# Decoder kernel: position-bias matmuls interleaved over row quarters and PSUM banks, and the residual stream held in eight fixed tiles

## The chip, the core and the metric

The kernel runs on one core of a Trainium2 chip. The core has five engines that work through their own instruction queues in order and meet at semaphores: TensorE (PE; its weight loads are shown apart as PEld), VectorE (DVE), ScalarE (ACT), GpSimd (POOL) and SyncE (SP), which here only issues DMAs. The metric is the device time of one execution in microseconds; lower is better. Three executions of the kernel before took 3527.88, 3530.78 and 3538.53 us (median 3530.78).

## What is computed

A two-layer decoder over 64 sequences of 128 positions with 256 features. Six blocks follow each other, each adding to the residual stream `x`:

```python
x = x + L0_attn(layernorm(x), ...)            # A: window-7 attention, 16 heads
x = x + L0_xattn(layernorm(x), ctx, mask, ...) # B: masked cross attention, no projections of q, k, v
x = x + L0_ffn(layernorm(x), ...)             # C: 64 slots, top-8 routing, GRU update of the slots
x = x + L1_attn(layernorm(x), ...)            # D: causal attention with a position bias
x = x + L1_xattn(layernorm(x), ctx, ...)      # E: cross attention
x = x + L1_ffn(layernorm(x), ...)             # F: ternary-weight FFN with a depthwise convolution
```

The position bias of D is one 128 x 128 table for each of 16 heads, the same for all sequences:

```python
rel = log(abs(c * (pos_t - pos_s)) + 1)
pos_norm = log(abs(c * max(pos_t, abs(512 * L_multiplier))) + 1) + 1e-6
h = relu((rel / pos_norm)[..., None] * w1[0] + b1)   # 32 hidden values for each pair (t, s)
bias = einsum('tsw,wh->hts', h, w2) + b2             # -inf where s > t
att = softmax(q @ k.T * scale + bias)
```

## The kernel before

All is float32, apart from the quantised operands of F. The 64 sequences are taken in 16 groups of four (`GB` = 4), so that a tile of the residual stream is [128 positions, 4, 256], 512 KB. Every stage reads the groups from DRAM and writes them back: A writes `ab`, B and C together write `cd`, D writes `de`, E writes `ef`, F writes the output. The class `Flow` (L61 to L80) does this. `reach(g)` makes a tile of the pool `xp` (six buffers, L1354) for each group up to `g` and issues its load on SP's queue (L77); `store(g)` issues the store there (L80). Weights and `ctx` are loaded on the same queue (L96, L578), a few broadcast rows on POOL's.

The program is not run in the order in which it is written. A scheduler places every instruction on its engine's queue by its own estimate of when its inputs are there and when buffers come free, with the order of the text as priority; after that each engine is strictly in order. So a load is placed as early as a buffer of its pool is free. With six buffers, the load of a group waits for the store of the group six before it.

Stage A (`stage_window`) works in groups. Between two of its groups it calls one preparation of a later stage at a time. One of them is `prep_fire`, which makes the bias table: `nd` holds, in each quarter of 32 partitions, the 32 hidden values for 32 of the 128 positions t and all 128 s. For each quarter q (L971) one PSUM bank is taken from the pool `ps`, 32 matmuls (L974) of a stationary 32 x 128 piece of `nd` by the moving 32 x 16 `w2` fill it, and four DVE additions (L980) move it to `bias_t`. POOL then masks it (L985), and 16 transposes (L989) make `bias_s`. A matmul in float32 runs as two instructions, so that L974 is 256 of them.

Beside this stands the window attention of A itself: `window_values` (L325) takes two tiles of two banks each from the pool `sc` (two buffers), fills them with the spread weights (L333), and DVE multiplies and sums (L339, L343).

Stage B (`stage_cross0`) is written for each sequence as `prep`, which normalises (`ln_stats`: L122 to L125, then `r` L617 and `qp` L623), and `attention_stage`, a software pipeline of half-steps shared by B, D and E: score bursts of 16 matmuls (L433, 32 instructions), exponentials on ACT (L456, L454), maxima on DVE (L460), transposes and values on PE (L471, L483, L495, L512), output (L165). In B the burst takes two row quarters for the scores of one sequence and the other two for the scores of another. Stage C, the slots, runs inside B's pipeline a step at a time (`Slots.tick`); its last additions to a group (L868) release the store to `cd`. D and E (`stage_attn`) project each group ahead of its use (`group_project`), and F (`stage_bitnet`) is a pipeline over groups of its own, with DVE, POOL and ACT in turn: `hs` times a scale on POOL (L1264), rounding on DVE (L1265), convolution on PE (L1210).

Of the kernel before, what the change touches and what calls it, by code (L numbers as in the profile page):

```python
# [10 lines left out]
F = mybir.dt.float32  # L11
# [5 lines left out]
D = 256  # L17
H = 16
DH = 16
S = 128  # L20
WIN = 7
SLOTS = 64
GB = 4
# [37 lines left out]
class Flow:  # L61

    def __init__(self, k, src, dst):
        self.k, self.src, self.dst = k, src, dst
        self.at = -1
        k.x = {}
        k.flow = self

    def reach(self, g):

        k = self.k
        while self.at < min(g, k.G - 1):
            self.at += 1
            k.x[self.at] = k.xp.tile([S, GB, D], F, tag="x", name="x")
            k.nc.sync.dma_start(out=k.x[self.at], in_=self.src[self.at])  # L77

    def store(self, g):
        self.k.nc.sync.dma_start(out=self.dst[g], in_=self.k.x[g])  # L80


def outside(k, name):
# [23 lines left out]
def psum(k):  # L107
    return k.ps.tile([128, 512], F, tag="ps", name="ps")


def psum2(k):
    return k.sc.tile([128, 2, 512], F, tag="sc", name="sc")
# [460 lines left out]

def load_group(k, pool, g):
    cx = pool.tile([S, GB, D], F, tag="cx", name="cx")
    k.nc.sync.dma_start(  # L578
        out=cx, in_=k.a["ctx"][g * GB : (g + 1) * GB].rearrange("b l d -> l b d")
    )  # L580
    return cx


def stage_cross0(k, w, wc):


    nc = k.nc
    with k.tc.tile_pool(name="wb", bufs=2) as wp, k.tc.tile_pool(name="wb1", bufs=1) as w1, \
            k.tc.tile_pool(name="wb3", bufs=3) as w3, k.tc.tile_pool(name="wc2", bufs=2) as c2:
        qps, kps, vas = [], [], []  # L590
        for i in range(2):
            qp = w1.tile([S, H, 32], F, name=f"qp{i}")
            nc.gpsimd.memset(qp, 0.0)
            nc.gpsimd.memset(qp[:, :, 17:18], 1.0)
            qps.append(qp)
            kp = w1.tile([S, H, 32], F, name=f"kp{i}")
            nc.gpsimd.memset(kp, 0.0)
            nc.gpsimd.memset(kp[:, :, 16:17], 1.0)
            kps.append(kp)
        for i in range(4):  # L600
            va = w1.tile([S, H, 32], F, name=f"va{i}")
            nc.gpsimd.memset(va, 0.0)
            nc.gpsimd.memset(va[:, :, 16:17], 1.0)
            vas.append(va)
        cxs = {0: load_group(k, wp, 0)}
        k.flow.reach(0)
        stats = {}

        def prep(bi):
            g, b = divmod(bi, GB)  # L610
            if b == 0:
                k.flow.reach(g + 1)
                if g + 1 < k.G:
                    cxs[g + 1] = load_group(k, wp, g + 1)
                mv, rs = ln_stats(k, wp, g)
                r4 = wp.tile([S, GB], F, tag="r4", name="r4")
                nc.vector.tensor_scalar(r4, rs, 0.25, None, ALU.mult)  # L617
                stats[g] = mv, r4
            mv, r4 = stats[g]
            mk = w.mask[:, bi : bi + 1]  # L620
            qp, kp, va = qps[b % 2], kps[b % 2], vas[b]
            xb = k.x[g][:, b, :]
            nc.vector.tensor_scalar(  # L623
                qp[:, :, 0:DH], xb.rearrange("p (h d) -> p h d", d=DH),
                mv[:, b, 0:1], r4[:, b : b + 1], ALU.subtract, ALU.mult,
            )
            xm = wp.tile([S, D], F, tag="xm", name="xm")
            nc.gpsimd.tensor_scalar(xm, w.bp, mk, None, ALU.mult)
            nc.gpsimd.tensor_tensor(xb, xb, xm, ALU.add)
            cv = cxs[g][:, b, :].rearrange("p (h d) -> p h d", d=DH)  # L630
            nc.gpsimd.tensor_copy(kp[:, :, 0:DH], cv)
            nc.gpsimd.tensor_copy(kp[:, :, 17], w.mbias[:, bi : bi + 1].to_broadcast([S, H]))
            nc.gpsimd.tensor_scalar(va[:, :, 0:DH], cv, mk, None, ALU.mult)
            t = Batch()
            t.qt = w3.tile([128, 4, S], F, tag="qt", name="qt")
            t.kt = w3.tile([128, 4, S], F, tag="kt", name="kt")
            for src, dst in ((qp, t.qt), (kp, t.kt)):
                p = psum(k)
                sf = src.rearrange("p h i -> p (h i)")
                for c in range(4):  # L640
                    nc.tensor.transpose(
                        p[:, c * S : (c + 1) * S], sf[:, c * 128 : (c + 1) * 128], k.ident
                    )
                nc.scalar.copy(dst, p.rearrange("p (c l) -> p c l", l=S))
            t.va, t.row_scale = va, mk

            def fin(y):
                nc.vector.scalar_tensor_tensor(xb, y, mk, xb, ALU.mult, ALU.add)

            t.fin = fin  # L650
            return t

        slots = Slots(k, wc, c2, w1)
        attention_stage(k, wp, w1, prep, w.wp, Heads(False), tick=slots.tick)
        slots.finish()

# [279 lines left out]
def prep_fire(k, pool):  # L936
    nc = k.nc
    bt = pool.tile([S, 4, 4, S], F, name="bias_t")
    bs = pool.tile([S, 4, 4, S], F, name="bias_s")
    with k.tc.tile_pool(name="firew", bufs=1) as cp:  # L940
        w1 = load(k, cp, "f_w1")
        b1 = load(k, cp, "f_b1")
        w2 = load(k, cp, "f_w2")
        b2 = load_row(k, cp, "f_b2")
        c = load_row(k, cp, "f_c")
        lm = load_row(k, cp, "f_l")
        thr = cp.tile([128, 1], F, name="thr")
        nc.scalar.activation(thr, lm, AF.Abs, scale=512.0)
        pn = cp.tile([128, 32], F, name="pn")
        nd = cp.tile([128, 32, S], F, name="nd")  # L950
        for q in range(4):
            sl = slice(32 * q, 32 * q + 32)
            nc.gpsimd.iota(
                pn[sl], [[1, 32]], base=32 * q, channel_multiplier=0,
                allow_small_or_imprecise_dtypes=True,
            )
            nc.gpsimd.iota(
                nd[sl], [[1, 32], [-1, S]], base=32 * q, channel_multiplier=0,
                allow_small_or_imprecise_dtypes=True,
            )  # L960
        nc.vector.tensor_scalar(pn, pn, thr[:, 0:1], None, ALU.max)
        nc.scalar.activation(pn, pn, AF.Abs, scale=c[:, 0:1])
        nc.scalar.activation(pn, pn, AF.Ln, bias=1.0)
        nc.vector.tensor_scalar(pn, pn, 1e-6, None, ALU.add)
        nc.vector.reciprocal(pn, pn)
        nc.scalar.activation(nd, nd, AF.Abs, scale=c[:, 0:1])
        nc.scalar.activation(nd, nd, AF.Ln, bias=1.0)
        nc.vector.tensor_tensor(nd, nd, pn.unsqueeze(2).to_broadcast([128, 32, S]), ALU.mult)
        nc.scalar.activation(nd, nd, AF.Relu, scale=w1[:, 0:1], bias=b1[:, 0:1])
        b2v = b2.rearrange("p (c r) -> p r c", r=4)  # L970
        for q in range(4):  # L971
            p = psum(k)
            for t in range(32):
                nc.tensor.matmul(  # L974
                    p[:, t * H : (t + 1) * H], nd[32 * q : 32 * q + 32, t, :],
                    w2[32 * q : 32 * q + 32, :], start=True, stop=True,
                )
            pv = p.rearrange("p (t c r) -> p r c t", c=4, r=4)
            for r in range(4):
                nc.vector.tensor_tensor(  # L980
                    bt[:, r, :, 32 * q : 32 * q + 32], pv[:, r],
                    b2v[:, r, :].unsqueeze(2).to_broadcast([S, 4, 32]), ALU.add,
                )
        btf = bt.rearrange("p r c l -> p (r c) l")
        nc.gpsimd.affine_select(btf, btf, [[0, 16], [1, S]], ALU.is_ge, NEG, 0, -1)  # L985
        for r in range(4):
            p = psum(k)
            for cc in range(4):
                nc.tensor.transpose(p[:, cc * S : (cc + 1) * S], bt[:, r, cc, :], k.ident)  # L989
            nc.scalar.copy(bs[:, r], p.rearrange("p (c l) -> p c l", l=S))  # L990
    return bt.rearrange("p r c l -> p r (c l)"), bs.rearrange("p r c l -> p r (c l)")
# [351 lines left out]
def decoder(tc, a):  # L1343
    k = Ctx()
# [6 lines left out]

    with ExitStack() as ctx:
        k.res = ctx.enter_context(tc.tile_pool(name="res", bufs=1))
        k.xp = ctx.enter_context(tc.tile_pool(name="xp", bufs=6))  # L1354
        k.dram = ctx.enter_context(
            tc.tile_pool(name="flow", bufs=1, space=bass.MemoryType.DRAM)
        )
# [3 lines left out]
        p = Ctx()  # L1361
# [143 lines left out]
```

## Time and profile before

| | us |
|---|---|
| median of three executions | 3530.78 |
| the profiled execution | 3546.0 |
| its span, first to last instruction | 3544.2 |
| mean granted TensorE clock of it | 0.906 of full speed |

Busy time of each engine by stage, from windows of the trace (the stages overlap a little at their ends, so that the borders are rounded):

| stretch, us | stage | PE | DVE | ACT | POOL | TensorE clock |
|---|---|---|---|---|---|---|
| 0 to 690 | A and preparations | 545.71 | 490.27 | 98.85 | 335.51 | 0.84 |
| 690 to 1626 | B with C | 756.73 | 575.23 | 383.34 | 329.72 | 0.90 |
| 1626 to 2330 | D | 624.78 | 622.47 | 286.60 | 62.47 | 0.95 |
| 2330 to 2925 | E | 558.73 | 356.99 | 289.37 | 59.72 | 0.99 |
| 2925 to 3544 | F | 444.38 | 508.46 | 252.54 | 215.90 | 0.85 |

No engine is busy all through any stage. A busy PE is not PE at its peak: its matmuls are pipelined and their ends are modelled. The granted clock is the share of full speed that TensorE got in a stretch. The page of a profile also has rows by line of the program ("busy, mean ns of one", then the idle time of the engine just before them and what ended it), and the chain of work that ended last, followed back from the last instruction.

### The profile page before, as it was taken

To read this page: it belongs to the slowest core of one execution; us is meant where nothing else is said; L and a number is where in the kernel's file an instruction comes from. 1 tells how busy PE (TensorE), PEld (TensorE's weight loads), DVE (VectorE), ACT (ScalarE), POOL (GpSimd) and SP (SyncE) were. 2 spreads that over 40 slices of the span, in tenths; PEclk is the share of its full clock that TensorE was granted. 3 is DMA by queue.
4 is the path that set the end of the run, shared out by engine and by line. 5 is a ranking of instruction groups with operands and counts; after the bars stand their busy time and mean duration, and the time that the engine had idled before them with its cause. 6 is when DMAs were issued, how large, how long until landed. Compare 5 with 4: busy or idle time off the path is not lost.

```text
span 3544.2 us, 65123 instructions
## 1 busy us (share of the span) xinstructions
PE 2930.3 (83%) x27738; PEld 1892.7 (53%) x27764; DVE 2553.4 (72%) x4875; ACT 1310.7 (37%) x2012; POOL 1003.3 (28%) x920
## 2 busy tenths in 40 slices
PE   5869888688888878877999999879999987777776
PEld 2445333365656656654666666657777763333333
DVE  6855787666666666657988899865656559888876
ACT  1111111044444444433444444335555544434442
POOL 6434555434333333312000000030101003334323
PEclk9867999789999999988999999999999998888887
DMA  4100010100101001000000000011111110001000
GB/s 129 60 12 12 36 36 24 54 13 19 37 19 37 25 31 37 13 30 19 25 25 25 25 25 25 25 49 38 55 37 55 38 44 8 33 24 36 24 12 24
DMA packets 59249, 115.20 MB, mean 33 GB/s; under 512 B 6496, under 2 KB 39664, under 8 KB 58704
## 3 DMA queue, kind: packets, MB, share of 16 engines
q1 hardware_dynamic: 58304, 109.29, 8.9%
q8 instruction: 219, 3.59, 0.4%
q0 software_dynamic: 656, 1.75, 0.2%
q14 instruction: 70, 0.57, 0.1%
HBM read 69.08 MB, written 41.94 MB: 31 GB/s over the span
## 4 chain that ended last, share of the span: by engine, by line
PE 40%; DVE 35%; POOL 9%; ACT 7%; DMA 5%; issue 4%; SPq 0%; POOLq 0%; DVEq 0%; ACTq 0%
PE sc L433 9%; PE ps L156 7%; DVE negmax L460 5%; PE ps L165 5%; DVE uq L1265 4%; PE ps L483 3%; DVE sb L447 3%; DVE e L453 3%; PE cv L1210 2%; DVE pv L339 2%; ACT e L454 2%; DVE oT L343 2%; PE ps L1045 2%; PE ps L471 2%; POOL pr L281 2%
## 5 line engine op out<-in xcount | busy, mean ns | idle before, releaser
L433 PE MATMUL sc<-kt,qt 32*128 32x128 f32 x6144 | 519.5, 297 | 152.6 <-DVE negmax L460 97.5
L433 PEld LDWEIGHTS sc<-kt,qt 32*128 32x128 f32 x6144 | 425.1, 196 | 331.4 <-DVE negmax L460 149.2
L433 PE MATMUL sc<-q,kt 32*128 32x128 f32 x6144 | 491.5, 295 | 5.2 <-DVE q L475 2.6
L433 PEld LDWEIGHTS sc<-q,kt 32*128 32x128 f32 x6144 | 407.2, 196 | 26.5 <-DVE rec L498 11.6
L460 DVE TENSOR_REDUCE negmax<-sc 128x8 f32<-128x1024 f32 x256 | 312.4, 1220 | 138.6 <-ACT e L456 133.6
L456 ACT ACTIVATE e<-sc 128x1024 f32<-128x1024 f32 x256 | 261.5, 1021 | 324.4 <-PE sc L433 324.0
L1210 PE MATMUL cv<-hp,taps 128*128 128x512 f32 x480 | 259.6, 684 | 63.7 <-DVE hp L1200 63.4
L281 POOL TENSOR_TENSOR pr<-pad,qt 128x896 f32<-128x896 f32 x128 | 244.9, 1945 | 191.8 <-ACT pad L268 184.4
L475 DVE TENSOR_TENSOR q<-ps,qt 128x512 f32<-128x512 f32 x192 | 131.9, 687 | 154.2 <-PE ps L471 154.2
L1264 POOL TENSOR_TENSOR hs<-hs,s2b 128x512 f32<-128x512 f32 x128 | 180.0, 1441 | 198.1 <-ACT s2b L1256 198.1
L454 ACT ACTIVATE e<-e 128x1024 f32<-128x1024 f32 x128 | 135.3, 1057 | 240.7 <-DVE e L453 240.7
L447 DVE TENSOR_TENSOR sb<-sc,bias_s 128x1024 f32<-128x1024 f32 x128 | 156.6, 1223 | 66.0 <-PE sc L433 66.0
L1210 PEld LDWEIGHTS cv<-hp,taps 128*128 128x128 f32 x480 | 97.8, 215 | 191.0 <-DVE hp L1200 94.3
L125 POOL TENSOR_TENSOR ln_rs<-ln_ve,expo 128x4 f32<-128x4 f32 x96 | 101.9, 1061 | 328.8 <-DVE ln_ve L124 198.3
L122 DVE BATCH_NORM_STATS2 ln_st<-x 128x6 f32<-128x256 f32 x384 | 153.4, 425 | 56.5 <-DMA x<-ab 29.8
L339 DVE TENSOR_TENSOR pv<-sc,pad 128x896 f32<-128x896 f32 x128 | 137.0, 1083 | 77.7 <-PE sc L333 77.6
L1013 POOL TENSOR_TENSOR x<-x,t_d_bo 128x1024 f32<-128x1024 f32 x16 | 37.6, 2353 | 469.4 <-DVE xn L132 469.4
L488 ACT COPY avs<-ps 128x512 f32<-128x512 f32 x192 | 112.2, 584 | 153.7 <-PE ps L483 153.7
L1265 DVE TENSOR_SCALAR uq<-hs 128x512 bf16<-128x512 f32 x128 | 151.4, 1233 | 8.6 <-POOL hs L1264 8.6
L453 DVE TENSOR_TENSOR e<-sc,bias_t 128x1024 f32<-128x1024 f32 x128 | 155.5, 1215 | 1.3 <-PE sc L433 1.3
L460 DVE TENSOR_REDUCE negmax<-sb 128x8 f32<-128x1024 f32 x128 | 154.9, 1210 | 0.0
L333 PE MATMUL sc<-fw,spread 32*128 32x448 f32 x512 | 111.4, 648 | 50.5 <-DVE fw L322 27.7
(329 smaller groups left out, 6448.6 us busy)
## 6 DMA issues: line engine op xcount, KB each, us to landing
cx<-in_ctx_dram SPq DMA_DIRECT2D x32, 512.0 KB, 4.2
x<-in_x_dram SPq DMA_DIRECT2D x16, 512.0 KB, 3.8
ab<-x SPq DMA_DIRECT2D x16, 512.0 KB, 2.6
x<-ab SPq DMA_DIRECT2D x16, 512.0 KB, 3.2
cd<-x SPq DMA_DIRECT2D x16, 512.0 KB, 2.8
x<-cd SPq DMA_DIRECT2D x16, 512.0 KB, 3.2
de<-x SPq DMA_DIRECT2D x16, 512.0 KB, 2.6
x<-de SPq DMA_DIRECT2D x16, 512.0 KB, 3.2
```

What stands on the lines that cost most here:

```text
L156: k.nc.tensor.matmul(out, w[:, kc, c0 : c0 + cn], rhsT[:, kc, n0 : n0 + n], start=(kc == 0), stop=(kc == 1),)
L281: k.nc.gpsimd.tensor_tensor(pr[:, c], shift_windows(t.kt, b, c), t.qt[:, c, b, :].unsqueeze(1).to_broadcast([128, WIN, S]), ALU.mult,)
L339: nc.vector.tensor_tensor(pv, bc[th][:, :, 0 : WIN * 64].rearrange("p c (l w) -> p c l w", w=WIN), shift_windows2(t.vt, b, th), ALU.mult,)
L433: k.nc.tensor.matmul(t[:, side * 2 + rr, c * S : (c + 1) * S], st[rows, c, :], mv[rows, c, :], start=True, stop=True,)
L447: nc.vector.tensor_tensor(sb, src, bias_s[:, hf * 2 : hf * 2 + 2, :], ALU.add)
L453: nc.vector.tensor_tensor(e, t[:, 2:4, :], bias_t[:, hf * 2 : hf * 2 + 2, :], ALU.add)
L454: nc.scalar.activation(e, e, AF.Exp)
L456: nc.scalar.activation(e, t[:, 2:4, :], AF.Exp)
L460: nc.vector.tensor_reduce(b.lay.extra(b.nm, hf * 2), src.rearrange("p r (c m) -> p r c m", m=S), AX.X, ALU.max, negate=True,)
L1210: nc.tensor.matmul(pc, w.taps[:, CONV_PE.index(j), t, :], hp[:, :, t : t + S], start=(t == 0), stop=(t == 2),)
L1264: nc.gpsimd.tensor_tensor(hs[:, j], hs[:, j], s2b, ALU.mult)
L1265: nc.vector.tensor_scalar(uq[:, j], hs[:, j], MAGIC, MAGIC, ALU.add, ALU.subtract)
```

## The change

The bias matmuls change their order: position t runs in the outer loop and the row quarter q in the inner one, and the four quarters write four different banks, which come from the pool `sc` as two tiles of two banks. The DVE additions of all four quarters follow after the last matmul. The residual stream gets eight fixed tiles of the resident pool, which all stages use in turn, in place of the pool `xp`. A store is noted in a list and issued by the next call of `reach`, behind its load, or with the last group. In stage B, `ctx` has three buffers in place of two.

```diff
     def __init__(self, k, src, dst):
         self.k, self.src, self.dst = k, src, dst
         self.at = -1
+        self.done = []
         k.x = {}
         k.flow = self
...
         while self.at < min(g, k.G - 1):
             self.at += 1
-            k.x[self.at] = k.xp.tile([S, GB, D], F, tag="x", name="x")
+            k.x[self.at] = k.xs[k.turn % len(k.xs)]
+            k.turn += 1
             k.nc.sync.dma_start(out=k.x[self.at], in_=self.src[self.at])
+        self.flush()
 
     def store(self, g):
-        self.k.nc.sync.dma_start(out=self.dst[g], in_=self.k.x[g])
+        self.done.append(g)
+        if g == self.k.G - 1:
+            self.flush()
+
+    def flush(self):
+        for g in self.done:
+            self.k.nc.sync.dma_start(out=self.dst[g], in_=self.k.x[g])
+        self.done = []
...
-def load_group(k, pool, g):
-    cx = pool.tile([S, GB, D], F, tag="cx", name="cx")
+def load_group(k, pool, g, bufs=None):
+    cx = pool.tile([S, GB, D], F, tag="cx", name="cx", bufs=bufs)
...
-        cxs = {0: load_group(k, wp, 0)}
+        cxs = {0: load_group(k, wp, 0, 3)}
...
-                    cxs[g + 1] = load_group(k, wp, g + 1)
+                    cxs[g + 1] = load_group(k, wp, g + 1, 3)
...
-        for q in range(4):
-            p = psum(k)
-            for t in range(32):
+        ps = [psum2(k) for _ in range(2)]
+        for t in range(32):
+            for q in range(4):
                 nc.tensor.matmul(
-                    p[:, t * H : (t + 1) * H], nd[32 * q : 32 * q + 32, t, :],
+                    ps[q // 2][:, q % 2, t * H : (t + 1) * H], nd[32 * q : 32 * q + 32, t, :],
                     w2[32 * q : 32 * q + 32, :], start=True, stop=True,
                 )
-            pv = p.rearrange("p (t c r) -> p r c t", c=4, r=4)
+        for q in range(4):
+            pv = ps[q // 2][:, q % 2].rearrange("p (t c r) -> p r c t", c=4, r=4)
             for r in range(4):
                 nc.vector.tensor_tensor(
                     bt[:, r, :, 32 * q : 32 * q + 32], pv[:, r],
...
-        k.xp = ctx.enter_context(tc.tile_pool(name="xp", bufs=6))
+        k.xs = [k.res.tile([S, GB, D], F, name=f"x{i}") for i in range(8)]
+        k.turn = 0
```

## Prediction

> **What bounds the kernel now.** I read the table of stages first: no engine is full anywhere, so each stage is set by waits, and I looked for those that the edits touch. First the row of the bias matmuls and the window of the trace in which they run. The columns of a window: length, then busy time with the number of instructions for PE, PEld, DVE, ACT and POOL, then the granted TensorE clock, the DMA share and GB/s.
>
> ```profile
> L974 PE MATMUL ps<-t_f_w,nd 32*128 32x16 f32 x256 | 52.1, 369 | 0.0
> 237.00:289.00 52.00, 52.00 (x260) 52.00 (x260) 2.65 (x12) 0.00 (x0) 0.00 (x0) 0.50 0.00 1
> ```
>
> For 52 us PE works through 256 small matmuls, one every 51.31 / 256 = 0.200 us, and DVE does 2.65 us of work, ACT and POOL none. The chain of waits has 51.31 us of L974 in one piece. This stretch is wholly on the path that sets the end. The clock stays at 0.50.
>
> Next, who waits for DMAs. The row of the layer norm statistics, then the chain of waits in one group of stage B (start, us, what), then windows from one `cd` store to the next.
>
> ```profile
> L122 DVE BATCH_NORM_STATS2 ln_st<-x 128x6 f32<-128x256 f32 x384 | 153.4, 425 | 56.5 <-DMA x<-ab 29.8 <-DMA x<-de 21.1 <-DMA x<-cd 2.9
> ...
> 905.38 2.91 DMA cd<-x
> 908.29 0.02 issue
> 908.30 3.11 DMA x<-ab
> 911.41 0.02 issue
> 911.44 1.41 DVE ln_st L122 x4
> ...
> 905.40:961.40 56.00, 47.32 (x542) 35.24 (x538) 35.81 (x97) 23.85 (x39) 20.48 (x28) 0.90 0.09 29
> 961.40:1014.30 52.90, 44.49 (x558) 33.48 (x550) 35.59 (x97) 23.75 (x39) 20.62 (x28) 0.97 0.09 31
> 1014.30:1072.30 58.00, 46.88 (x550) 34.88 (x546) 35.92 (x98) 23.87 (x39) 20.47 (x28) 0.91 0.09 28
> ...
> 1412.00:1462.90 50.90, 44.52 (x554) 33.49 (x554) 34.04 (x87) 23.76 (x39) 19.55 (x27) 0.97 0.06 22
> ```
>
> The load of a group waits for the store of the group six before it, about 6 to 8 us for both, and DVE, in order, stands at L122 for it: in B ten times, 29.8 us. Behind it are queued the next `negmax` (L460), and behind that the score burst of PE. Where store and load take 5.8 us, PE keeps a clock of 0.97 and the group takes 53; where they take 6 to 8, PE idles long enough to fall to 0.5 for some us, and the group takes 56 to 58. The window from 1412 has no such wait (all groups are loaded): 50.9.
>
> **The bias matmuls.** What a matmul costs when four row quarters take turns in four banks, the kernel shows: the score burst of B has that form (timeline, same columns of time).
>
> ```profile
> 1024.75 0.42 PE L433 MATMUL sc<-kt,qt 32*128 32x128 f32 x1
> 1024.76 0.42 PE L433 MATMUL sc<-q,kt 32*128 32x128 f32 x1
> 1024.77 0.42 PE L433 MATMUL sc<-kt,qt 32*128 32x128 f32 x1
> 1024.77 0.42 PE L433 MATMUL sc<-q,kt 32*128 32x128 f32 x1
> 1024.96 0.42 PE L433 MATMUL sc<-kt,qt 32*128 32x128 f32 x1
> ```
>
> Four start together and the next four 0.21 us later, at a clock of 0.50; seven such fours start within 1.28 us, 0.213 each. At full clock (897.67 to 897.90) a four takes 0.11. L974 loads the same 32 x 128 weights, so 256 / 4 x 0.213 = 13.6 us in place of 51.3.
>
> Here a rule speaks for more. The Trainium skill, "TensorE: Matmul & The Clock Gate", Part 1, says that some 3.4 us of sustained activity release the half clock; then 64 x 0.11 = 7.0 us. The row says otherwise: 52 us without a gap stayed at 0.50. I take 13.6 and keep 7.0 as the good end. Part 3 of the page has 3.07 for fourfold row packing, an estimate of 51.3 / 3.07 = 16.7, the bad end; four equal row quarters in the trace are nearer than a moving side of 512. No gain at all is excluded by the fours above.
>
> What is added: now all 16 additions (L980, 4 in 0.88 us) follow the last matmul. The two `sc` tiles belong to the window values too, so in the built order the first pair of L333 goes from ahead of the bias matmuls to behind them and waits for the eight additions of one tile, 1.76 us, then its own 1.83: DVE's L339 starts 3.6 us after the last matmul, before 0.9. In return the first bias matmul no longer stands behind that pair: it can start when `nd` is there (235.93), not at 236.97. Sum: before, L339 at 290.0; after, 235.9 + 13.6 + 3.6 = 253.1. Mask and transposes behind the additions move as much (235.9 + 13.6 + 3.5 against 290.03). **Gain 37** (34 to 43). The `sc` tiles are free at 220, so the new wait costs PE nothing.
>
> **Eight tiles, stage B.** The load now waits for the store eight groups back. In the built order the four L122 of a group stand 42 DVE instructions behind the last addition that this store waits for, before 8; a group has 92 in 51 us, so 42 are some 23 us, against 6 to 8 of DMA. The wait is gone, and they stand beside `r` (L617), where DVE waits for POOL anyway (36.4 us in 15 times): one fits there, three of 0.33 come on top. What is late next is that pipeline itself, as in the window of 50.9, so 52 a group. Ten groups took 1412.0 - 847.2 = 564.8; 10 x 52 = 520: **gain 45**. Bounds: if every group only becomes like the fast ones, 10 x 53 = 530, 35; if the idle alone goes, 30; all as the last, 56.
>
> **D and E.** Here the scheduler still puts L122 just behind the store: 16 DVE instructions behind the last addition, before 11, and the five more are short (four L123 and L124, some 0.45 us). So of 2.1 us in each of ten waits of E about half goes (these five also no longer stand between L122 and `negmax`). PE is at clock 1.00 and busy 34.4 of 35.5 us a group in E, and 34.8 a group without the wait: all of it would be 7, I take **4**. In D the waits are 2.9 us in all. Its groups take 41.0 at clock 1.00 and 43.5 at 0.92, by two PE gaps of 1.7 us behind DVE, which the change leaves there; I take **2**, between -10 and +17 (nine groups at 41.0 in place of 386.1).
>
> **F.** No wait for a load before or after. But its tiles come earlier, and the order on DVE and ACT turns: the maximum L1166 (1.13 us) goes from behind the rounding, which is on the chain, to a place ahead of it, and four copies of ACT (L1154, 1.28 us) now partly precede `s2b` (L1256), which starts POOL. One each way: **0**, between -16 and +16 (1 us in 16 groups of 37.5).
>
> **What costs nothing.** The noted stores: in the built order each store still stands directly ahead of the load of its tile, so SP issues them when DVE is ready, as before; the list changes nothing. The third `ctx` buffer: in both orders the `ctx` load ahead of each `cd` store waits for the same POOL instruction (SP waits 622.8 us for L633, until some 4 us before the store); if it came later, the 23 us of slack would be eaten first. Two more loads at the start (8 tiles ahead) stand before weights that E needs at 2330. The order on POOL changes in a few L125, on PE by the bias and some ten matmuls.
>
> **Sum.** 37 + 45 + 4 + 2 + 0 = 88. From the profiled execution 3546.0 - 88 = 3458. That run was 0.4% above the median 3530.8; on the median's scale 3530.8 - 88 = **3443**.
>
> **Rivals.** (1) Only the bias counts, chance 0.12: in B the wait at L122 is replaced by an equal one at L617, POOL or the slots, because B's chain is all latency. For: DVE waits everywhere in B. Against: the windows of 50.9 and 52.9. Time 3531 - 37 - 6 = 3488. (2) The clock is released too, 0.10: bias at full clock (43), B at 51 (55), D at 41.0 (17), E 7: 3409. For: the clock in B and D falls only by a hair. Against: 0.50 for 52 us. (3) Slower, 0.04: the turned order of F. If an extra convolution burst of 5.1 us and the copies' 1.3 lie open in each of 16 groups, that is 16 x 6.4 = 102, against 88: 3531 + 14 = 3545. It decides from 5.5 us a group. Against: DVE, POOL and PE there keep their neighbours but for a few short instructions. (4) That eight tiles don't free the loads is excluded by the built order for B, and is what I count for D and E. The forecast itself: 0.74.
>
> **Range.** The likeliest case's low end has 43 + 55 + 7 and 15 of D and F, 3411; its high end 34 + 35 + 0 - 15, 3477. With rival 1 inside: 3405 to 3492. A measurement of this kernel tells 0.3%, 10.6 us, from no change. Faster 0.94, same 0.02, slower 0.04.
>
> **What would show it.** L974 should have a start-to-start of about 0.053 us and some 14 us in all; the wait for `x<-ab` at L122 near zero; the groups of B at 52 with a clock of 0.95 or more; `x<-de` still there at 10 to 15 us; F's group near 37.5. I am wrong if the fours do not overlap (L974 at 40 or more), if B's groups stay at 56 with a wait elsewhere, or if F's group grows.

## The result and the profile after

The changed kernel takes 3491.96 us (median of four executions, 3486.41 to 3502.48), the kernel before 3532.70 beside it: a ratio of 0.9887, 95% interval 0.9858 to 0.9917. It is faster, by 41 us. The forecast was 88. The two profiled executions differ by 51 us (spans of 3544.2 and 3493.1), since the profiled one of before is 13 us above its median and that of after 3 us; executions of one kernel spread by some 10 us either way with their mean granted clock (0.905 to 0.911 for the kernel before in one series, 3549.95 to 3529.20 us). Where the places of a gain are told below, they are those of profiled executions; where a kernel is called faster, it is by medians.

First the places. These are windows of the changed kernel, cut at the stores: nine B groups, the first D group, the other D groups, the first E group, ten E groups. Columns: start and end, length, busy time (and number of instructions) of PE, PEld, DVE, ACT and POOL, granted TensorE clock, DMA share, GB/s.

```profile
806.40:1285.90 479.50, 412.56 (x4875) 307.97 (x4874) 319.08 (x862) 213.97 (x351) 181.77 (x252) 0.94 0.09 31
1545.00:1646.50 101.50, 86.45 (x890) 58.03 (x890) 88.52 (x160) 37.62 (x52) 15.49 (x10) 0.90 0.03 12
1646.50:2249.30 602.80, 537.19 (x6798) 379.00 (x6790) 532.01 (x771) 249.55 (x349) 43.04 (x31) 0.97 0.08 28
2249.30:2344.80 95.50, 78.50 (x889) 56.64 (x890) 65.49 (x135) 39.05 (x56) 26.45 (x28) 0.91 0.10 34
2344.80:2719.80 375.00, 346.47 (x4883) 258.82 (x4881) 233.66 (x424) 181.12 (x261) 33.58 (x20) 0.99 0.13 44
```

From the windows of the kernel before, cut at the same stores, the first and the last two of these stretches:

```profile
847.20:1355.80 508.60, 417.43 (x4886) 311.41 (x4878) 322.09 (x865) 214.56 (x351) 184.52 (x252) 0.92 0.09 29
2324.00:2416.00 92.00, 76.55 (x889) 55.27 (x890) 62.88 (x126) 38.98 (x56) 26.37 (x27) 0.93 0.11 36
2416.00:2771.40 355.40, 344.40 (x4882) 256.43 (x4881) 216.36 (x431) 180.62 (x261) 33.64 (x20) 1.00 0.14 46
```

All stretches set side by side, in us, and what each gained, before less after:

| stretch | before | after | gain |
|---|---|---|---|
| A with the bias table, to its last store | 682.7 | 643.3 | 39.4 |
| to the first `cd` store | 164.5 | 163.1 | 1.4 |
| B, nine groups | 508.6 | 479.5 | 29.1 |
| rest of B, and C | 264.5 | 259.1 | 5.4 |
| first D group | 98.0 | 101.5 | -3.5 |
| D, the others | 605.7 | 602.8 | 2.9 |
| first E group | 92.0 | 95.5 | -3.5 |
| E, ten groups | 355.4 | 375.0 | **-19.6** |
| E, the last five | 147.7 | 147.7 | 0 |
| F | 625.1 | 625.6 | -0.5 |

The expected gain is there in A and, for the greater part, in B; E gives back 23 us of it. What is to be read in E's line is the DVE column. Fewer instructions (424 against 431) are busy for longer (233.66 against 216.36): 17.3 us of work have come up that no added instruction does, and PE's own busy time has hardly moved. An instruction of DVE must have become slower. No wait shows that: the row of the layer norm statistics on the page, which before had 56.5 us of waiting, has 2.6 left.

```profile
L133 DVE BATCH_NORM_STATS2 ln_st<-x 128x6 f32<-128x256 f32 x384 | 152.2, 426 | 2.6 <-DMA x<-cd 0.6
```

It is `ln_ve`, a small instruction of the layer norm. These are its windows over the ten E groups (L124 in the kernel before, then L135 in the changed one; start and end, length, busy time of these instructions alone, clock, DMA share, GB/s): ten times the same instruction, 18.3 us more.

```profile
2416.00:2771.40 355.40, 1.70 (x10) 1.00 0.14 46
2344.80:2719.80 375.00, 19.98 (x10) 0.99 0.13 44
```

Over the whole program its row went from 52.1 to 70.4 us, but that sum is no measure: another profiled execution of the changed kernel (e6_after, below) has 60.2, with the same 20 us in these ten groups.

The timeline of DVE in one E group of the changed kernel (start, us, what):

```profile
2420.38 1.37 DVE L143 TENSOR_SCALAR xn<-x,ln_mv,ln_rs 128x256 f32<-128x256 f32 x4
2421.79 0.38 DVE L134 BATCH_NORM_AGGREGATE ln_mv<-ln_st 128x2 f32<-128x6 f32 x4
2422.20 2.00 DVE L135 TENSOR_SCALAR ln_ve<-ln_mv 128x4 f32<-128x4 f32 x1
2424.11 0.68 DVE L486 TENSOR_TENSOR q<-ps,qt 128x512 f32<-128x512 f32 x1
2424.71 1.21 DVE L471 TENSOR_REDUCE negmax<-sc 128x8 f32<-128x1024 f32 x1
```

The same of POOL:

```profile
2421.83 2.34 POOL L1025 TENSOR_TENSOR x<-x,t_e_bo 128x1024 f32<-128x1024 f32 x1 [33.70 <-DVE xn L143]
2424.34 1.02 POOL L136 TENSOR_TENSOR ln_rs<-ln_ve,expo 128x4 f32<-128x4 f32 x1 [0.17 <-DVE ln_ve L135]
```

`ln_ve` adds 1e-5 to 128 x 4 numbers. It takes 2.00 us, and ends when POOL's `x + bo` ends (2424.20 and 2424.17). That POOL operation is released by the last `xn`, so whatever DVE has directly behind `xn` runs beside it. Behind `ln_ve` stand `q` and `negmax`, and behind `negmax` PE, which is idle for 2.53 us ahead of its next scores at 2425.97. In the kernel before, the same instruction is at another place in the same queue:

```profile
2452.11 1.37 DVE L132 TENSOR_SCALAR xn<-x,ln_mv,ln_rs 128x256 f32<-128x256 f32 x4
2453.40 0.68 DVE L475 TENSOR_TENSOR q<-ps,qt 128x512 f32<-128x512 f32 x1
2454.00 1.22 DVE L460 TENSOR_REDUCE negmax<-sc 128x8 f32<-128x1024 f32 x1
...
2457.91 0.75 DVE L122 BATCH_NORM_STATS2 ln_st<-x 128x6 f32<-128x256 f32 x2 [2.08 <-DMA x<-de]
...
2459.70 0.17 DVE L124 TENSOR_SCALAR ln_ve<-ln_mv 128x4 f32<-128x4 f32 x1
```

There `q` and `negmax` follow `xn` at once, beside the same POOL operation (2453.56 to 2455.91), and are not slower for it; `ln_ve` comes four us after POOL is done and takes 0.17 us. In the order of the changed kernel, eleven of E's sixteen `ln_ve` stand right behind `xn`, with only the four `ln_mv` between; before, one did.

This is the theory of the experiments, T: **DVE's `ln_ve` stands still beside POOL's `x + bo`; eight tiles move it there, because the scheduler reckons with earlier loads.** With six tiles one of the sixteen stands there (e7_sixE, e9_six_late and e11_sixDE below). That the scheduler's estimate of the loads is the reason is an inference; other numbers of tiles were not run. The Trainium skill, "SBUF — State Buffer", section "Who interferes with whom", describes such a thing: VectorE and GpSimd share one pair of SBUF ports, the one that comes first holds it for its whole instruction, and a `tensor_scalar` from SBUF to SBUF is among the operations that may ask for it, while a `tensor_reduce` is not. The rows above fit that, with 2.00 us in place of 0.17 for `ln_ve`, and 1.22 beside that operation and 1.21 away from it for `negmax`; the ports themselves no trace here shows. The rival R: E's groups are longer because transfers or PE's order have changed. PE's order is the same in the two traces: between the stores of the ten groups 4880 matmuls follow each other, tile for tile as before.

### The profile page after: what moved, and what is told of

Same layout as the page of the kernel before. It is cut to its first block, busy times and chain, and to the rows that moved or that the text cites. A ratio compares the mean times of both kernels' runs of the same rounds, so it can differ in the third digit from the quotient of the medians.

```text
span 3493.1 us, 65076 instructions
## 1 busy us (share of the span) xinstructions
PE 2893.9 (83%) x27764; PEld 1845.9 (53%) x27764; DVE 2568.4 (74%) x4875; ACT 1311.4 (38%) x2012; POOL 998.4 (29%) x920
## 4 chain that ended last, share of the span: by engine, by line
PE 41%; DVE 37%; POOL 9%; ACT 7%; issue 4%; DMA 1%; SPq 0%; POOLq 0%; DVEq 0%; ACTq 0%
PE sc L444 10%; PE ps L167 7%; DVE negmax L471 6%; PE ps L176 5%; PE ps L494 4%; DVE uq L1277 4%; DVE sb L458 3%; DVE e L464 3%; PE cv L1222 2%; DVE xn L143 2%; DVE pv L350 2%; ACT e L465 2%; DVE oT L354 2%; PE ps L482 2%; PE ps L1057 2%
## 5 line engine op out<-in xcount | busy, mean ns | idle before, releaser
L1025 POOL TENSOR_TENSOR x<-x,t_e_bo 128x1024 f32<-128x1024 f32 x16 | 37.5, 2344 | 443.1 <-DVE xn L143 443.1
```

## The experiments

Ten kernels ran, in three series, each beside its own runs of the kernel before.

**e1_bias and e2_tiles: the two parts alone.** The first is the kernel before with the edit of the bias matmuls, the second all the rest of the change.

> The kernel before with the new order of the position-bias matmuls alone. All theories: the 256 bias matmuls take 13.6 us instead of 52, so 38.6 us less, a ratio near 0.989, and stages B, D, E, F as before (E groups 35.5 us apart). Theory T (E's new order gives back what B gains): the full change is only about 10 us faster than this kernel. The theory on record (bias 37 of 88): the full change is 51 us faster than this one.

> The full change with the old order of the bias matmuls: tiles in turn, late stores and third context buffer alone. Theory T: B gains some 33 us (53.2 us a group), E loses 18 to 20 us (37.2 us a group, because its 128x4 ln_ve takes 2 us beside POOL's x+bo), D and F the same: 12 to 15 us faster than before, ratio 0.996. The theory on record: 51 us faster, ratio 0.9855. A third, that B's gain was only the profiled execution's: no difference.

Measured: bias alone 3499.04 us, ratio 0.9890 (0.9872 to 0.9908); the rest alone 3540.42 us against 3540.59, ratio 1.0002 (0.9986 to 1.0018). So, by the medians, the whole of the 41 us is the bias edit's. The trace of the rest alone has what T says of the stages (ten B groups 528.9 us, ten E groups 379.9, all ten `ln_ve` there 2.00 us). Its span is 12 us below that of before, but the profiled execution of before was 13 us above its median, and the median of the rest alone is not lower. T was right in place; its 12 to 15 us are not in the medians, which show no gain and no loss. The mean granted clock was 0.905 over 14 executions against 0.908 over the 19 of before. A straight line through those 19 gives 1.8 us for each 0.001 of the clock, so an estimate of 5 us goes with that difference; whether the lower clock comes from the PE gaps in E or from elsewhere, this pair doesn't show.

**e3_veE and e5_nobo: `ln_ve` away from DVE, and POOL away from `ln_ve`.** The first moves E's `ln_ve` to POOL's queue. The second leaves out the addition of the output bias in E.

```diff
-    nc.vector.tensor_scalar(ve, mv[:, :, 1], 1e-5, None, ALU.add)
+    (eng or nc.vector).tensor_scalar(ve, mv[:, :, 1], 1e-5, None, ALU.add)
...
-            layernorm(k, wp, g, xn)
+            layernorm(k, wp, g, xn, nc.gpsimd if cross else None)
```

```diff
-            nc.gpsimd.tensor_tensor(
-                k.x[g], k.x[g], w.bo.unsqueeze(1).to_broadcast([S, GB, D]), ALU.add
-            )
+            if not cross:
+                nc.gpsimd.tensor_tensor(
+                    k.x[g], k.x[g], w.bo.unsqueeze(1).to_broadcast([S, GB, D]), ALU.add
+                )
```

> The changed kernel with stage E's 128x4 ln_ve on POOL, behind which ln_rs already is, instead of VectorE. Theory T: VectorE no longer stands still 1.8 us at that instruction, the first ten E groups go from 37.2 to 34.8-35.5 us apart, the whole is 17 to 24 us faster than the changed kernel (some 3470 us). Rival R (E's groups are longer because eight tiles start loads and stores at other moments, or because of PE's order): E stays at 37.2 us a group and the time at 3492 us.

> The changed kernel without the addition of the output bias bo to x in stage E (POOL's 128x1024 x+bo is left out there, so the output lacks that bias); VectorE's order in E is the same as in the changed kernel. Theory T: without POOL's 2.35 us operation beside it, ln_ve takes 0.17 us instead of 2.0, though it stands at the same place, and E's groups are 34.8-35.2 us apart: about 3470 us. Rival R (order or DMA, not POOL beside VectorE): ln_ve or the group stays long, 37 us a group.

Measured: 3478.61 us, ratio 0.9820 (0.9796 to 0.9845), and 3484.73, ratio 0.9845 (0.9825 to 0.9864). Ten E groups take 352.4 and 354.4 us. In the second, all 422 DVE instructions that start in the ten groups stand in the order of the changed kernel, and `ln_ve` at the very same place is short again (timeline of DVE):

```profile
2390.98 0.38 DVE L134 BATCH_NORM_AGGREGATE ln_mv<-ln_st 128x2 f32<-128x6 f32 x4
2391.39 0.17 DVE L135 TENSOR_SCALAR ln_ve<-ln_mv 128x4 f32<-128x4 f32 x1
2391.47 0.69 DVE L486 TENSOR_TENSOR q<-ps,qt 128x512 f32<-128x512 f32 x1
```

That takes the order by itself, and the transfers, out as the cause: only the neighbour on POOL is gone. In the first, POOL does both, in turn (timeline of POOL), and `ln_ve` costs it 0.23 us:

```profile
2426.79 2.35 POOL L1025 TENSOR_TENSOR x<-x,t_e_bo 128x1024 f32<-128x1024 f32 x1 [31.52 <-DVE xn L143]
2429.11 0.23 POOL L135 TENSOR_SCALAR ln_ve<-ln_mv 128x4 f32<-128x4 f32 x1
2429.42 1.04 POOL L136 TENSOR_TENSOR ln_rs<-ln_ve,expo 128x4 f32<-128x4 f32 x1
```

R falls for E. Both came out above the 3470 us expected; in both traces another stage, D, was longer than in the changed kernel's trace (616.8 and 609.8 us from its first store to its last against 602.8, at a clock of 0.94 and 0.96 against 0.97).

**e6_after, e7_sixE and e9_six_late: which edit brings it, on one chip.** The changed kernel again; with six tiles in E only; and with six tiles everywhere (all of the change but the eight tiles).

```diff
-            k.x[self.at] = k.xs[k.turn % len(k.xs)]
+            k.x[self.at] = k.xs[k.turn % self.n]
...
-        Flow(k, de, ef)
+        Flow(k, de, ef, 6)
```

```diff
-            k.x[self.at] = k.xs[k.turn % len(k.xs)]
-            k.turn += 1
+            k.x[self.at] = k.xp.tile([S, GB, D], F, tag="x", name="x")
...
-        k.xs = [k.res.tile([S, GB, D], F, name=f"x{i}") for i in range(8)]
+        k.xp = ctx.enter_context(tc.tile_pool(name="xp", bufs=6))
```

> The changed kernel once more, on the chip of this group of runs, to set beside the others. Theory T: its ratio to before is that of the first measurement, 0.989, and the same as the bias order's alone (0.989): the tiles add nothing in the median. E's first ten groups at 37.2 us.

> The changed kernel with six tiles in turn in stage E only, eight elsewhere. With six, the scheduler puts E's ln_ve back where it was, away from POOL's x+bo (one group of sixteen directly behind xn instead of eleven). Theory T: ln_ve 0.17 us, the wait for x<-de back at about 2 us a group, E groups at 35.5, 15 to 18 us faster than the changed kernel. Rival R (E is longer for another reason, such as bias or late stores): E stays at 37.2 us.

> All of the change but the eight tiles: six tiles from a pool as before, with the new bias order, the late stores and the third context buffer. Theory T: the late stores and the third buffer change nothing, the groups of the cross stage stay at 56 us with the wait for x<-ab at some 30 us, E at 35.5: the time of the bias order alone, ratio 0.989. Rival: the stores behind the next load already take the wait away: cross groups at 53, ratio 0.98.

| | median us | ratio to before | interval | ten B groups | ten E groups |
|---|---|---|---|---|---|
| the change (e6_after) | 3507.37 | 0.9924 | 0.9898 to 0.9951 | 528.8 | 375.1 |
| six tiles in E (e7_sixE) | 3477.22 | 0.9853 | 0.9824 to 0.9882 | 529.8 | 357.1 |
| six tiles everywhere (e9_six_late) | 3497.64 | 0.9907 | 0.9879 to 0.9935 | 562.1 | 356.7 |

Ten B groups took 564.8 us in the kernel before. With six tiles the late stores and the third context buffer change nothing: `x<-ab` is waited for as before.

```profile
L132 DVE BATCH_NORM_STATS2 ln_st<-x 128x6 f32<-128x256 f32 x384 | 147.0, 408 | 59.8 <-DMA x<-ab 27.4
```

So B's gain is the eight tiles' and E's loss too, and by the medians the two together bring nothing over six tiles (3507.37 against 3497.64, with intervals that overlap). Six tiles in E bring the ten waits for `x<-de` back (22.8 us on the page of e7_sixE), and the stage is 18 us shorter all the same: the wait that the change removed in E cost less than the instruction that took its place. The gain over the changed kernel was larger than expected (30 us between the medians, against 15 to 18), and the changed kernel came out 15 us higher here than at first, which is not explained; its profiled execution was the lowest of six.

**e8_veP and e10_veDE: `ln_ve` on POOL in all stages, and in D and E alone.** The second edit is shown against e3_veE.

```diff
-    nc.vector.tensor_scalar(ve, mv[:, :, 1], 1e-5, None, ALU.add)
+    nc.gpsimd.tensor_scalar(ve, mv[:, :, 1], 1e-5, None, ALU.add)
```

```diff
-            layernorm(k, wp, g, xn, nc.gpsimd if cross else None)
+            layernorm(k, wp, g, xn, nc.gpsimd)
```

> The changed kernel with ln_ve on POOL in all stages. Theory T: E as in the run with ln_ve on POOL in E alone (35.2 us a group); in the window stage, where 11 of 16 ln_ve took 2 us beside POOL, VectorE is freed of some 16 us in all, of which at most half shows, since its groups wait on more than VectorE; in the cross stage ln_rs comes 0.1 to 0.2 us later a group. In all 20 to 28 us faster than the changed kernel. A rival: ln_ve now queues on POOL behind xm, va and the convolution's work, and the cross and last stages lose more than the window stage gains: 3490 us or more.

> The changed kernel with ln_ve on POOL in stages D and E. Theory T: E as in the run with ln_ve on POOL in E alone (35.2 us a group); of the first D group's 101.5 us (97 with six tiles) some 1 to 4 us come back, since up to four ln_ve of 1.0 to 2.0 us stand there beside POOL's x+bo; D's later groups unchanged. Ratio to before 0.981 to 0.985. Rival: D's start is longer because the layer norms of two more loaded groups stand ahead of its first scores on VectorE; then it stays at 101 us.

In all stages: 3487.29 us, 0.9873 (0.9839 to 0.9906), not better than in E alone. E is as expected (352.8), A hardly shorter (551.1 against 553.0 us from its first store to its last; kernels with the same A spread from 550.2 to 557.7), and ten B groups take 543.9 in its trace, where the other kernels with eight tiles have 526.6 to 533.4; its profiled execution was also the slowest of its six, at a clock of 0.92 in B. In these B groups DVE waits 36.9 us for POOL's `ln_rs`, against 29.4 in the changed kernel: 7.5 us, half or more of the difference if all of it lies on the path. Whether the rest is the lower clock is open. T had expected that some 16 us are freed in A and up to half of them show; that is a miss: the 2 us that `ln_ve` took there were not what A's groups waited for.

In D and E: **3460.68 us (3458.38 to 3462.82), 0.9780 (0.9760 to 0.9801)**, which is the lowest ratio of all and 77 us below before. The windows of its first D group, the first E group and ten E groups:

```profile
1542.00:1637.00 95.00, 81.45 (x892) 54.90 (x893) 83.40 (x153) 37.61 (x52) 16.93 (x16) 0.96 0.04 12
2241.00:2333.00 92.00, 77.12 (x889) 55.58 (x890) 53.52 (x127) 38.94 (x56) 27.31 (x33) 0.93 0.11 36
2333.00:2686.00 353.00, 344.41 (x4888) 256.79 (x4890) 213.30 (x414) 182.03 (x261) 35.86 (x30) 1.00 0.15 46
```

95.0, 92.0 and 353.0 us, against 101.5, 95.5 and 375.0 in the changed kernel: 32 us less, and more than expected at D's start (6.5 against 1 to 4). The wait for `x<-de` is seen again, 13.4 us on its page, since DVE no longer arrives late at it (the changed kernel has 0.2).

**e11_sixDE: eight tiles to the end of C, six in D and E.** As e7_sixE, with `Flow(k, cd, de, 6)` as well.

> The changed kernel with eight tiles in turn up to stage C and six in D and E. The rival of the run before (two more loaded groups ahead of D's first scores): D's first group back at 97 us, E at 35.5 us a group with some 2 us a group of waiting for x<-de, B's groups at 53 as with eight tiles; 4 us faster than six tiles in E alone, ratio 0.983 to 0.985. If D's start is ln_ve's: it stays at 101 us.

Measured: 3474.37 us, 0.9815 (0.9789 to 0.9841); ten B groups 533.5, ten E groups 356.2 with 21.9 us of waits for `x<-de`. Its first D group takes 98.0 us, as in the kernel before; it is 101.5 in the changed kernel, 101.4 with six tiles in E alone, 95.0 with `ln_ve` on POOL in D and E. So the 3.5 us that the change added to D's start go with the two tiles more. What DVE has more to do there is the statistics of two more loaded groups, ahead of D's scores: the windows of `ln_st` in the first D group, before and after, differ by eight instructions and 3.1 us.

```profile
1620.30:1718.30 98.00, 8.32 (x23) 0.95 0.03 12
1545.00:1646.50 101.50, 11.42 (x31) 0.90 0.03 12
```

`ln_ve` did not add to it: its six there are as long before as after (5.75 and 5.76 us, four of them beside `x + bo`). That `ln_ve` on POOL takes away 6.5 us with those groups still there is a gain on what the kernel before had lost already. E's start is the same case: eight `ln_st` more, 2.9 us, `ln_ve` 12.74 us both before and after, 92.1 us with six tiles in E, and 91.2 to 92.9 with eight where `ln_ve` or `x + bo` is moved out of the way. The intervals of this kernel and of e7_sixE overlap.

## Why the prediction was wrong

The sum was 37 + 45 + 4 + 2 + 0.

- **The bias matmuls (37): right.** The chain of the changed kernel has them in 13.86 us where 13.6 was forecast, at the clock of 0.50 that the row was taken from; the 7.0 us of a full clock did not come. The 16 additions follow in 3.25 us, and the window multiplication starts 3.7 us after the last matmul (forecast 3.6). A is 39.4 us shorter, though 4.8 of that are in the trace of e2_tiles too, which has the old order; the edit alone gave 41.6 us in the medians of its series.

```profile
236.94 13.86 PE sc L985 x254
250.80 0.02 issue
250.83 1.68 DVE bias_t L992 x8
```

- **Stage B (45): right in mechanism, 12 us too large.** The wait for `x<-ab` is gone and nothing took its place (DVE stands idle 178.6 us of the ten groups, 206.9 before), but they take 532.0 us, not 520: 564.8 - 532.0 = 33. Other traces of eight tiles have 526.6 to 533.4, e8_veP aside. The term that was too small is the 52 us a group, which I set near one window at the end of the stage. The groups are 53.2 at a clock of 0.94, as the fast ones before were, and the gain is about the 29.8 us that DVE had waited. The lower bounds, 30 and 35, were the estimate to take: what a wait is worth is the wait.
- **Stage E (4): the step that failed.** I saw in the built order that "the five more are short (four L123 and L124, some 0.45 us)", and priced them by what they take alone. Four of the five are short. The fifth, `ln_ve`, came to stand beside POOL's `x + bo` and takes 2.0 us there, ten times on the path, so the ten groups lost 19.6 us in place of gaining 4. The price was not hidden: the trace of before has `ln_ve` at a median of 1.6 us in A, and its mean over the program is 542 ns where alone it takes 170. E's start lost another 3.5 us by the statistics of two more loaded groups, a term that the sum did not have. With `ln_ve` on POOL, 3 of the 4 us are there (352.4 and 352.5 us for ten groups, against 355.4 in the kernel before) and the waits for `x<-de` are at 12.7 and 13.4 us, within the forecast 10 to 15; in the changed kernel itself they are gone, against the sign that I had named.
- **Stage D (2):** -0.6 in the traces, within the bounds. Its start lost 3.5 us, by the statistics of two more groups, as in E; the later groups won 2.9.
- **F (0), the stores and the context buffer (0): right.** F's window is the same within 0.5 us; e9_six_late shows the other two (ten B groups at 562.1 us without the eight tiles).

In the traces the forecast lacks 37 us: 27 of E with its start, 9 of B with C (45 less 35.9), 3 of D, less 2 that A gave beyond it. That `ln_ve` beside POOL is what made most of it is shown, by four kernels that part the two in different ways (on POOL in E, on POOL in D and E, `x + bo` left out, six tiles in E) and whose ten E groups all end 18 to 23 us lower. With the one instruction of D and E moved, the same change gives 77 us. The rival "only the bias counts", 3488 us, came nearest in time, and only by taking it in did the stated range, 3405 to 3492, reach the 3491.96 measured. That was luck: B's wait was not replaced in B, its gain was given back in E.

Two things stay open: why eight tiles with `ln_ve` on DVE show no gain at all in the medians when the profiled executions show 4 (the change against e1_bias) to 12 us (e2_tiles against before), and a part of what e8_veP loses in B.

## What to carry to other kernels

When a change moves buffers, compare the built order of each engine, and for every short DVE instruction that moves, look at what POOL does beside its new place: an instruction is priced by its neighbours, not by its mean. If the busy time of an engine rises while its instruction count doesn't, look for one instruction whose duration has become that of another engine's operation. And take for a removed wait the wait itself, not the best window elsewhere in the stage.

## What the runs showed of the hardware

A `tensor_scalar` of 128 x 4 on DVE takes 0.17 us alone and 2.00 us when it starts 0.37 us into a 2.34 us `tensor_tensor` on POOL; it is counted as busy, not as waiting, and no view names POOL as its releaser. Where POOL has one operation behind the other, it stands through all of them: at the start of E, before and after, one `ln_ve` takes 6.95 us beside a string of POOL operations, mostly memsets, and ends within 0.03 us of the last (after: 2253.09 to 2260.04, POOL to 2260.01). `bn_stats` and `bn_aggr` on SBUF tiles, and `tensor_reduce`, `tensor_tensor` and `reciprocal` with an operand in PSUM, kept their times within 0.04 us beside `x + bo`. On POOL, in turn behind `x + bo`, the small operation costs 0.23 us. PE kept its clock of 0.50 through 13.9 us of bias matmuls without a gap, as it had through 52.
